# Two of the last head's four softmax tiles turned by DMA instead of by TensorE, in a two-layer graph attention kernel

## The chip, the core and the metric

The kernel runs on one core of a Trainium2 chip. The metric is the device time of one execution in microseconds (us), as a median over several runs. TensorE (PE in the profile, its weight loads PEld), VectorE (DVE), ScalarE (ACT), GpSimd (POOL) and SyncE (SP) each work through their own list of instructions in order; SP here does nothing but issue DMAs. A wait on another engine or on a DMA holds up everything behind it on the same engine.

## What is computed

Two graph attention layers over 512 nodes and 16,896 edges, a residual and a normalisation. Cut to what matters:

```
def gat_layer(x, W, a_s, a_d, b, edges, concat):
    h = (x @ W).reshape(n, H, C)
    alpha_s, alpha_d = (h * a_s).sum(-1), (h * a_d).sum(-1)
    e = leaky_relu(alpha_s[src] + alpha_d[dst], 0.2)
    e = exp(e - segment_max(e, dst)[dst])
    alpha = e / (segment_sum(e, dst)[dst] + 1e-16)
    return segment_sum(h[src] * alpha, dst) + b

h   = elu(gat_layer(x, W1, ..., concat=True))   # 8 heads of 768
out = gat_layer(h, W2, ..., concat=True)        # 1 head of 768
return layernorm(x + out)
```

The kernel handles the edges densely: it counts the edges between each pair of nodes once, and a head's attention is then a 512x512 matrix, softmaxed row by row with the counts as weights, and multiplied with the head's features.

## The kernel before

**Tiles.** The 512 nodes are four tiles of 128 partitions. A softmax tile `q[t]` is 128 destinations x 512 sources, 32-bit floats. The product with the features wants sources on the partitions, so each of the four tiles has to be turned into its columns of the matrix `PT` (128 x 4 x 512).

**Order of the work.** The order on every engine is written out by hand; no scheduler moves anything. The loop at L833 runs seven times. Pass h multiplies head h's features with its attention (`mixed`, L742), applies the ELU, multiplies the result with head h's rows of W2 and adds that to the sum of layer two (`second`, L333). Beside this last product it makes the softmax of head h+1, and after it, except in the last pass, the features of head h+2. The products are split into halves with seven block products instead of eight (P1, P2, P6, P7, P4, P5, P3), each for two pieces of 128 rows. One piece is six matmul records of 128x384 in the trace, so each step n = 2 to 6 of L871 to L902 is twelve of them (m0, then m1, L305) and two VectorE evictions (e0, e1, L363).

**The softmax of a tile**, spread over these steps: `lift` (ACT, L452), `leak` (DVE, L456), `rank` (DVE row maximum, L461, then ACT exponential, L463), `weigh` (DVE, L667 to L673: times the counts, row sum, reciprocal, scaled).

**Two ways to turn a tile.** `turn` (L676) has TensorE transpose the four 128x128 blocks into a PSUM tile (L679; pool `tr`, two buffers), and ACT copies that to `PT` (L680). `turn_out` (L685) has ACT copy the tile apart into a plane of upper and a plane of lower half words (L687, tile `nr`, two buffers), and SP issues one DMA transpose of the 16-bit planes into a tile `zr` (L689, three buffers). `turn_in` (L691) has ACT interleave the half words of `zr` into `PT` (L692). Heads 0 to 6 and layer two use turn_out and turn_in for all four tiles, with the turn_in some steps later. The last head (number 7, made in pass h = 6, `last` in the code) uses `turn` for all four: tile 0 between the two pieces of step 4, tile 1 in step 5, tile 2 in step 6, and tile 3 ahead of the last two matmul records of step 6.

**What follows.** After that pass come, in program order, the loads of x (four DMAs on SP, L95) and of b2 (one on SP, L936), which are used by the last stage (L1027). Then `aggregate` (L706) multiplies the last head's features with `PT`: 48 matmul records of 128x512 (L710), each column group followed by ACT and DVE work, then `second` for the last head, layer two's own softmax, its product (L1039) and the normalisation. The first matmul of L710 waits for ACT's last write to `PT`.

Of the kernel before, what the change touches and what calls it, by code (L numbers as in the profile page):

```python
# [36 lines left out]
def gat_pass(  # L37
# [45 lines left out]
    def row_bcast(ap_row):  # L83
        return bass.AP(tensor=ap_row.tensor, offset=ap_row.offset, ap=[[0, P], [1, D]])
# [36 lines left out]
    def load_w1(h, slot="w2"):  # L121
        return load_w(W1, h, slot, w1[:, h * D:(h + 1) * D])

    def load_w2(h, slot="w1"):
        return load_w(W2, h, slot, w2[h * D:(h + 1) * D, :])

    def load_a(h, a_s, a_d):
        A[h] = []
        for name, a in (("a_s", a_s), ("a_d", a_d)):
            v = wpool.tile([P, D], F32, name=name)  # L130
            nc.sync.dma_start(v, row_bcast(a))
            A[h].append(v)
# [147 lines left out]
    def left(aT, s):  # L280
        a11, a12 = aT[:, :HK, :HN], aT[:, HK:, :HN]
        a21, a22 = aT[:, :HK, HN:], aT[:, HK:, HN:]
        tt = nc.vector.tensor_tensor
        return dict(P1=a11, P2=a12, P3=s[:, 2], P4=a22, P5=s[:, 0], P6=s[:, 1], P7=a21), [
            lambda: tt(s[:, 0], a21, a22, op=ALU.subtract),
            lambda: tt(s[:, 1], s[:, 0], a11, op=ALU.subtract),
            lambda: tt(a21, a11, a21, op=ALU.subtract),
            lambda: tt(s[:, 2], a12, s[:, 1], op=ALU.add),
        ]
# [23 lines left out]
    def half_logits(h, t):  # L313
        return [lambda al=al, a=a, sign=sign: nc.vector.scalar_tensor_tensor(
            scr, HS[h][:, t, :], sign, a, op0=ALU.mult, op1=ALU.mult, accum_out=al[:, t:t + 1])
            for al, a, sign in zip(AL[h], A[h], (1.0, -1.0))]
# [132 lines left out]
    def lift(h, t):  # L449

        q = qpool.tile([P, N], F32, name="q")
        nc.scalar.activation(q, BC[h][:, :N], AF.Identity, bias=AL[h][1][:, t:t + 1], scale=-1.0)  # L452
        return q
# [21 lines left out]
    if not general:  # L475
# [99 lines left out]
        for n, batch in enumerate(batches):  # L575
# [29 lines left out]
            if n + 1 == len(batches):  # L605
                spread(0)
                q = [lift(0, t) for t in range(NT)]
# [11 lines left out]
    else:  # L619
# [26 lines left out]
        q = [lift(0, t) for t in range(NT)]  # L646
# [17 lines left out]
    def weigh(q, t, scale=True):  # L664

        den = small.tile([P, 1], F32, name="den")
        nc.vector.scalar_tensor_tensor(q, q, 1.0, cnt[:, t, :], op0=ALU.mult, op1=ALU.mult,  # L667
                                       accum_out=den)
        rden = small.tile([P, 1], F32, name="rden")
        nc.vector.tensor_scalar(rden, den, EPS_DEN, None, op0=ALU.add)  # L670
        nc.vector.reciprocal(rden, rden)
        if scale:
            nc.vector.tensor_scalar(q, q, rden, None, op0=ALU.mult)  # L673
        return rden

    def turn(q, t):  # L676
        ps = tr.tile([P, 512], F32, name="tr")
        for s in range(NT):
            nc.tensor.transpose(ps[:, s * P:(s + 1) * P], q[:, s * P:(s + 1) * P], ident)  # L679
        nc.scalar.copy(PT[:, :, t * P:(t + 1) * P], ps[:, :N].rearrange("p (s d) -> p s d", d=P))  # L680
# [4 lines left out]
    def turn_out(q, t):  # L685
        apart = work.tile([P, N], F32, name="nr").bitcast(U16)
        nc.scalar.copy(apart.rearrange("p (h n) -> p h n", h=2), q.bitcast(U16).rearrange("p (n h) -> p h n", h=2))  # L687
        parted[t] = work.tile([P, N], F32, name="zr", bufs=3).bitcast(U16)
        nc.sync.dma_start(parted[t].rearrange("p (j d) -> p j d", d=P), apart, transpose=True)  # L689

    def turn_in(t):  # L691
        nc.scalar.copy(PT.rearrange("p s n -> p (s n)").bitcast(U16).rearrange("p (s n h) -> p s n h", s=NT, h=2)[  # L692
            :, :, t * P:(t + 1) * P, :], parted.pop(t).rearrange("p (h s d) -> p s d h", h=2, s=NT))
# [124 lines left out]
    def attended(k):  # L818


        b1_, b2_ = (wpool.tile([P, HK, HALF], F32, name=f"w2t{j}").rearrange("p k n -> p (k n)") for j in (2, 4))
        nc.sync.dma_start(b1_[:, :D], w2[(H - 1) * D + k * P:(H - 1) * D + (k + 1) * P, :])
        nc.sync.dma_start(b2_[:, :D], row_bcast(a_src2[0]))
        for b, cols in ((b2_, L), (b1_, R)):
            nc.sync.dma_start(b[:, D:], row_bcast(a_dst2[0])[:, cols])

        def times(cols, a, sign, out):
            return lambda: nc.vector.scalar_tensor_tensor(
                scr[:, cols], b1_[:, cols], sign, a, op0=ALU.mult, op1=ALU.mult, accum_out=out[:, k:k + 1])
        return [times(slice(0, D), b2_[:, :D], 1.0, V[:, :, 0]), times(L, b2_[:, D:], -1.0, V[:, :, 1]),  # L830
                times(R, b1_[:, D:], -1.0, V2)]

    for h in range(H - 1):  # L833
        if h + 2 < H:
            load_w1(h + 2)()
        else:
            A[H] = []
            for j, a in ((2, a_src2[0]), (4, a_dst2[0])):
                v = wpool.tile([P, HK, HALF], F32, name=f"w2t{j}").rearrange("p k n -> p (k n)")[:, :D]
                nc.sync.dma_start(v, row_bcast(a))  # L840
                A[H].append(v)
            last_sum = load_w2(H - 1, "w2")
        GA, gsums = left(gT, gS)
        finish = mixed(h, AA, BB, besides + [p for t in ((0, 1) if h else (0, 1, 3)) for p in half_logits(h + 1, t)])
        besides = []
        if h + 2 < H:
            load_a(h + 2, a_src1[h + 2], a_dst1[h + 2])
            attend = attended(h)
        pairs = second(h, GA, B2)
        for m, _ in pairs[:2]:  # L850
            m()
        pairs[0][1]()
        for f in finish:
            f()
        gsums[0]()
        pairs[1][1]()
        gsums[1]()
        if pending:
            pending.pop(0)()
        spread(h + 1)  # L860
        pairs[2][0]()
        gsums[2]()
        pairs[3][0]()
        gsums[3]()
        if pending:
            pending.pop(0)()
        pairs[2][1]()
        pairs[3][1]()
        last = h + 2 == H
        q = [lift(h + 1, 0)]  # L870
        for n in range(2, 7):  # L871
            (m0, e0), (m1, e1) = pairs[2 * n:2 * n + 2]
            m0()
            if not last:
                m1()
            if n < 6:
                leak(q[n - 2])
                rank(q[n - 2], n - 2)
            if n < 5:
                q.append(lift(h + 1, n - 1))  # L880
            if last:

                if n > 3:
                    turn(q[n - 4], n - 4)
                if n == 6:
                    weigh(q[3], 3)
                m1(lambda: turn(q[3], 3) if n == 6 else None)
            if not last and n == 6:
                turn_in(0)
                weigh(q[2], 2)  # L890
                turn_out(q[2], 2)
            e0()
            if last and 2 < n < 6:
                weigh(q[n - 3], n - 3)
            if not last and 3 < n < 6:
                weigh(q[n - 4], n - 4)
                turn_out(q[n - 4], n - 4)
            if not last and n == 6:
                weigh(q[3], 3)
                turn_out(q[3], 3)  # L900
                load_w2(h + 1)()
            e1()  # L902
        if h + 2 < H:
            B_, sums = right(W1[h + 2], "w2")
            pairs = projection(h + 2, XA, B_)
            for n in range(14):
                pairs[n][0]()
                if n == 0:
                    turn_in(1)
                    for f in attend:  # L910
                        f()
                    B2, sums2 = right(W2[h + 1], "w1")
                if n in (1, 3):
                    sums[n // 2]()
                if n == 1:
                    AA, sums3 = left_sums(h + 1)
                pairs[n][1]()
                if n in (2, 4):
                    turn_in(1 + n // 2)
                if n == 5:  # L920
                    BB, sums3 = right_sums()
                if 1 <= n < 9:
                    sums3.pop(0)()
                if n in (9, 10):
                    sums2.pop(0)()
                if n in (11, 13):
                    logits(h + 2, HS[h + 2], 2 + (n - 11) // 2)
        else:
            last_sum()
            B2, sums2 = right(W2[H - 1], "w1")  # L930
# [65 lines left out]
    q, rden = [lift(H, 0)], []  # L996
# [96 lines left out]
```

## Time and profile before

| | |
|---|---|
| median of 3 runs | 650.80 us (650.75 to 650.86) |
| profiled execution, its own time | 650.37 us |
| its span from first to last instruction | 648.6 us |
| busy PE / DVE / ACT / POOL | 98% / 80% / 43% / 7% of the span |
| DMA share in 549 to 557 us / 557 to 569 us | 0.03 / 0.08 |
| steps n = 4 to 6 of pass h = 6 on PE | 555.43 to 568.98 us |

Rows of the timeline are: start in us, length in us, engine, line, operation, output<-inputs, shapes, count, and in brackets the idle time of the engine just before and what ended it. Neighbouring instructions of one kind are merged in a row. A matmul's length contains its way through the array, so several overlap; what a group costs TensorE is read from the distance between the starts. PEclk is the granted TensorE clock, 1.00 in all stretches around the change.

### The profile page before, as it was taken

What the parts mean: (1) busy time and instruction counts of PE and PEld (TensorE: products, weight loads), DVE (VectorE), ACT (ScalarE), POOL (GpSimd) and SP (SyncE); (2) the same over time, 40 slices, a digit from 0 to 9 for tenths busy, and PEclk for the clock granted to TensorE, in tenths of its full rate; (3) what the DMA queues carried; (4) which work ended last, traced back from release to release, by engine and by line L of the source; (5) the groups of instructions that cost most, each with busy time, mean ns of one, the idle gap of its engine ahead of it and who ended that gap; (6) DMA issues with size and microseconds to landing.
All of it is one profiled execution on the core that took longest, in us unless ns stands there. A gap on an engine that the chain in (4) does not pass through costs nothing.

```text
span 648.6 us, 7216 instructions
## 1 busy us (share of the span) xinstructions
PE 637.7 (98%) x2383; PEld 405.0 (62%) x2383; DVE 519.6 (80%) x1141; ACT 277.3 (43%) x482; POOL 48.3 (7%) x90
## 2 busy tenths in 40 slices
PE   8999999999999999999999999999999999999995
PEld 4544586556765586556765586556755586644553
DVE  7989989977779677877779687877779687876775
ACT  6774744530726045430726045430726045243440
POOL 1310020011000110011000110011000110000000
PEclk9999999999999999999999999999999999999999
DMA  9993499197806792196806792196706892000122
GB/s 318 328 203 86 75 327 292 35 256 207 202 0 153 170 277 97 33 260 200 205 1 149 174 277 98 33 258 204 202 1 153 218 254 97 25 1 1 29 61 76
DMA packets 77640, 97.95 MB, mean 151 GB/s; under 512 B 37094, under 2 KB 60446, under 8 KB 77598
## 3 DMA queue, kind: packets, MB, share of 16 engines
q1 hardware_dynamic: 63934, 75.80, 37.5%
q0 software_dynamic: 12976, 20.65, 18.4%
q10 hardware_dynamic: 688, 0.98, 0.4%
q8 instruction: 21, 0.34, 0.2%
q14 instruction: 21, 0.17, 0.1%
HBM read 85.09 MB, written 1.57 MB: 134 GB/s over the span
## 4 chain that ended last, share of the span: by engine, by line
PE 96%; ACT 1%; DMA 1%; DVE 1%; issue 0%; SPq 0%
PE mm L305 64%; PE mm L764 20%; PE mm L710 3%; PE mm L1039 3%; PE held L305 2%; PE tr L543 1%; DMA w<-in_L_gnn_W_dram 1%; ACT os L515 1%; PE bc L446 0%; PE bc L543 0%; PE tr L963 0%; PE tr L679 0%; ACT xT L205 0%; DVE os L517 0%; PE bc L985 0%
## 5 line engine op out<-in xcount | busy, mean ns | idle before, releaser
L305 PE MATMUL mm<-w,gT 128*128 128x384 f32 x288 | 97.5, 488 | 0.0
L305 PE MATMUL mm<-w,xT 128*128 128x384 f32 x264 | 88.2, 488 | 0.0
L305 PEld LDWEIGHTS mm<-w,gT 128*128 128x128 f32 x288 | 54.0, 190 | 35.2 <-issue 1.6
L305 PEld LDWEIGHTS mm<-w,xT 128*128 128x128 f32 x264 | 50.0, 190 | 35.4 <-ACT os L515 0.8
L768 ACT COPY u<-mm 128x256 f32<-128x256 f32 x21 | 7.8, 372 | 142.0 <-PE mm L764 142.0
L463 ACT ACTIVATE q<-q,nmax 128x512 f32<-128x512 f32 x36 | 25.8, 721 | 89.8 <-DVE nmax L461 89.8
L764 PE MATMUL mm<-PT,hs 128*128 128x256 f32 x252 | 61.4, 380 | 0.0
L305 PE MATMUL mm<-w1t,gS 128*128 128x384 f32 x180 | 60.7, 486 | 0.0
L305 PE MATMUL mm<-w2t,xS 128*128 128x384 f32 x168 | 56.6, 487 | 0.0
L764 PEld LDWEIGHTS mm<-PT,hs 128*128 128x128 f32 x252 | 47.9, 190 | 8.3 <-issue 0.4
L363 DVE TENSOR_TENSOR h<-h,mm 128x384 f32<-128x384 f32 x72 | 39.7, 551 | 14.6 <-PE mm L305 14.0
L305 PEld LDWEIGHTS mm<-w1t,gS 128*128 128x128 f32 x180 | 34.2, 190 | 23.5
L305 PEld LDWEIGHTS mm<-w2t,xS 128*128 128x128 f32 x168 | 31.9, 190 | 22.4 <-ACT q L452 0.4
L764 PE MATMUL mm<-pS,gS 128*128 128x256 f32 x168 | 43.3, 380 | 0.0
L687 ACT COPY nr<-q 128x1024 uint16<-128x1024 uint16 x32 | 33.4, 1044 | 22.9 <-DVE q L673 15.8
L692 ACT COPY PT<-zr 128x1024 uint16<-128x1024 uint16 x32 | 37.1, 1160 | 2.0 <-DMA zr<-nr 2.0
L764 PEld LDWEIGHTS mm<-pS,gS 128*128 128x128 f32 x168 | 31.9, 190 | 4.7 <-DVE pS L737 0.4
L305 PE MATMUL mm<-w,gS 128*128 128x384 f32 x96 | 32.6, 486 | 0.0
L305 PE MATMUL mm<-w1t,gT 128*128 128x384 f32 x96 | 32.5, 488 | 0.0
L305 PE MATMUL mm<-w,xS 128*128 128x384 f32 x96 | 32.5, 488 | 0.0
L106 POOL DMA_DIRECT2D w1t<-in_L_gnn_W_dram x7 | 8.9, 1267 | 311.3 <-DVE hs L727 97.8
L363 DVE TENSOR_TENSOR u<-u,mm 128x384 f32<-128x384 f32 x28 | 15.4, 553 | 19.0 <-PE mm L305 18.7
(189 smaller groups left out, 1086.1 us busy)
## 6 DMA issues: line engine op xcount, KB each, us to landing
w<-in_L_gnn_W_dram SPq DMA_DIRECT2D x90, 384.0 KB, 6.1
w<-in_L_gnn_W_dram POOLq DMA_DIRECT2D x16, 576.0 KB, 9.5
w2t<-in_L_gnn_W_dram SPq DMA_DIRECT2D x10, 576.0 KB, 4.9
w1t<-in_L_gnn_W_dram SPq DMA_DIRECT2D x9, 576.0 KB, 4.6
w2t<-in_L_gnn_W_dram POOLq DMA_DIRECT2D x8, 576.0 KB, 9.8
w1t<-in_L_gnn_W_dram POOLq DMA_DIRECT2D x7, 576.0 KB, 8.7
a_s<-in_L_gnn_a_src_dram SPq DMA_DIRECT2D x8, 384.0 KB, 3.7
a_d<-in_L_gnn_a_dst_dram SPq DMA_DIRECT2D x8, 384.0 KB, 4.1
```

What stands on the lines that cost most here:

```text
L106: nc.gpsimd.dma_start(t1, upper[:, :, R], accum_op=ALU.add)
L305: nc.tensor.matmul(ps[:, :HALF], A_[p][:, k, i * P:(i + 1) * P], B_[p][:, k, :], start=start and k == 0, stop=k == HK - 1, skip_group_chec ...
L363: nc.vector.tensor_tensor(a, a, ps, op=ALU.subtract if p == "P7" else ALU.add)
L463: nc.scalar.activation(q, q, AF.Exp, bias=nmax, scale=-1.0)
L515: nc.scalar.activation(o, nodes, AF.Sign, bias=nidx[:, c:c + 1])
L543: nc.tensor.matmul(cps[t][r:r + B, :N], od[:, at[c] + b - blocks[c][0], :], h_, start=todo[b] == hits[b], stop=todo[b] == 1, tile_position ...
L687: nc.scalar.copy(apart.rearrange("p (h n) -> p h n", h=2), q.bitcast(U16).rearrange("p (n h) -> p h n", h=2))
L692: nc.scalar.copy(PT.rearrange("p s n -> p (s n)").bitcast(U16).rearrange("p (s n h) -> p s n h", s=NT, h=2)[:, :, t * P:(t + 1) * P, :], p ...
L710: nc.tensor.matmul(ps[:, :N], HS[h][:, s, c * P:(c + 1) * P], PT[:, s, :], start=(s == 0), stop=(s == NT - 1))
L764: nc.tensor.matmul(bank[p][:, :HN], A_[p][:, k, c * P:(c + 1) * P], B_[p][:, k, :], start=over is None and k == 0, stop=k == 1, skip_group ...
L768: nc.scalar.copy(u, part("P1"))
L1039: nc.tensor.matmul(ps[:, :cols.stop - cols.start], PT[:, s, t * P:(t + 1) * P], h2[:, s, cols], start=(s == 2), stop=(s == 1))
```

## The change

Tiles 0 and 1 of the last head are turned by turn_out and turn_in; tiles 2 and 3 stay with `turn`. turn_out of tile 0 follows its `weigh` in step 3, that of tile 1 in step 4; turn_in of tile 0 stands in step 5, that of tile 1 in step 6, ahead of `turn` of tile 2. Nothing else is edited. The two DMA transposes thereby stand ahead of the loads of x and b2 in SP's list.

```
             if last:
-                if n > 3:
-                    turn(q[n - 4], n - 4)
+                if n > 4:
+                    turn_in(n - 5)
+                if n == 6:
+                    turn(q[2], 2)
                 if n == 6:
                     weigh(q[3], 3)
                 m1(lambda: turn(q[3], 3) if n == 6 else None)
...
             e0()
             if last and 2 < n < 6:
                 weigh(q[n - 3], n - 3)
+                if n < 5:
+                    turn_out(q[n - 3], n - 3)
```

## The prediction

> **What bounds the kernel now.** I read the page first: busy shares, then the chain that ended last.
>
> ```profile
> span 648.6 us, 7216 instructions
> ...
> PE 637.7 (98%) x2383; PEld 405.0 (62%) x2383; DVE 519.6 (80%) x1141; ACT 277.3 (43%) x482; POOL 48.3 (7%) x90
> ...
> PE 96%; ACT 1%; DMA 1%; DVE 1%; issue 0%; SPq 0%
> ```
>
> TensorE is the bound: 98% busy, 96% of the chain. Time taken off its queue counts in full, unless what it feeds on is late. So next comes the timeline of PE around the four turns, where the distance between starts gives the price of each.
>
> ```profile
> 551.56 4.03 PE L305 MATMUL mm<-w,gT 128*128 128x384 f32 x12
> 555.43 2.10 PE L305 MATMUL mm<-w1t,gT 128*128 128x384 f32 x6
> 557.36 0.60 PE L679 MATMUL tr<-ident,q 128*128 128x128 f32 x4
> 557.80 2.10 PE L305 MATMUL mm<-w1t,gT 128*128 128x384 f32 x6
> 559.74 2.10 PE L305 MATMUL mm<-w1t,gS 128*128 128x384 f32 x6
> 561.67 0.60 PE L679 MATMUL tr<-ident,q 128*128 128x128 f32 x4
> 562.11 2.10 PE L305 MATMUL mm<-w1t,gS 128*128 128x384 f32 x6
> ...
> 567.71 0.60 PE L679 MATMUL tr<-ident,q 128*128 128x128 f32 x4
> 568.15 0.81 PE L305 MATMUL mm<-w,gS 128*128 128x384 f32 x2
> 568.98 20.87 PE L710 MATMUL mm<-PT,hs 128*128 128x512 f32 x48
> ```
>
> The reader is to see three things. A step without a turn lasts 555.43 - 551.56 = 3.87 us, so 0.3225 us a record. A turn puts the next row 0.44 us later (557.36 to 557.80, 561.67 to 562.11). And the last two records start at 568.15 and need 0.645, so L710 could start at 568.80; it starts at 568.98, 0.18 late. The timeline of ACT tells why:
>
> ```profile
> 558.80 0.57 ACT L680 COPY PT<-tr 128x512 f32<-128x512 f32 x1
> 561.86 0.72 ACT L463 ACTIVATE q<-q,nmax 128x512 f32<-128x512 f32 x1 [2.49 <-DVE nmax L461]
> 562.49 0.57 ACT L680 COPY PT<-tr 128x512 f32<-128x512 f32 x1
> 566.62 0.58 ACT L680 COPY PT<-tr 128x512 f32<-128x512 f32 x1 [3.56 <-PE tr L679]
> 568.35 0.58 ACT L680 COPY PT<-tr 128x512 f32<-128x512 f32 x1 [1.15 <-PE tr L679]
> ```
>
> Tile 3's copy starts 0.64 us after its transposes start (567.71), ends at 568.93, and L710 follows 0.05 later. This entry, ACT's last write to PT, is the place that the change can spoil.
>
> **What goes.** Two turns leave TensorE: 2 x 0.44 = **0.88 us**. Two L680 copies of 0.57 us leave ACT; nobody waited for these two.
>
> **What comes.** Per tile one L687 copy, one DMA transpose and one L692 copy. The trace has 32 of each, from other heads:
>
> ```profile
> L687 ACT COPY nr<-q 128x1024 uint16<-128x1024 uint16 x32 | 33.4, 1044 | 22.9 <-DVE q L673 15.8
> L692 ACT COPY PT<-zr 128x1024 uint16<-128x1024 uint16 x32 | 37.1, 1160 | 2.0 <-DMA zr<-nr 2.0
> ```
>
> ```profile
> L689 SPq DMA_TRANSPOSE zr<-nr x32: 1232/1233/1360, 68.8 to 620.0; - x32
> ...
> DMA to landing us min/median/max: 3.0/3.1/3.5
> ```
>
> ACT so gets 2 x (1.04 + 1.16 - 0.57) = 3.3 us more work. In 549 to 569 us it is busy for 6.7 us of 20, so there is room; what matters is the order. In the changed list ACT does: L687 of tile 0, exponential of tile 2, lift of tile 3, L687 of tile 1, exponential of tile 3, L692 of tile 0, L692 of tile 1, then the two L680. I walk through it:
>
> - Tile 0 is scaled by DVE until 555.28 + 0.49 = 555.77. L687 runs 555.80 to 556.85. Behind it waits the exponential of tile 2, whose row maximum is only there at 557.56: free. SP issues at 556.87; landed by 559.9 to 560.4.
> - Tile 1 is scaled until 559.15 + 0.48 = 559.63. L687 runs 559.66 to 560.71. Behind it waits tile 3's exponential, whose maximum comes at about 561.45 (561.83 before, as DVE gets ahead by 0.3 at 559.94, see below): free. SP issues at 560.73; landed at **563.8 to 564.2**.
> - L692 of tile 0: 562.2 to 563.35. L692 of tile 1 waits for its landing: 563.8 to 565.0, at the latest 565.4.
> - On PE step 5 now starts at 559.30 and step 6 at 563.17. Turn 2 starts at 563.17 + 1.94 = 565.11, so its copy can't start before 565.75. Turn 3 starts at 565.55 + 4 x 0.3225 = 566.84, its copy at 567.48, and that ends at 568.06.
>
> So L710 starts at **568.10 instead of 568.98**: the 0.88 us arrive whole, and the 0.18 us ahead of L710 stay as they are. ACT's slack: for tile 3's copy to start on time, tile 2's copy (0.57) must start by 566.91 and L692 of tile 1 (1.16) by 565.75. A landing up to 5.0 us after the issue costs nothing; from there each us costs one.
>
> **DVE beside it.** VectorE has nothing added, but it must keep pace. The eviction at 559.94 had waited 0.30 for PE; it now starts at 559.63, where DVE is simply finished with tile 1. From there DVE runs without a gap: tile 2 is scaled by 563.64 (wanted at 565.11), the eviction that the second half of step 6 writes after runs 563.64 to 564.2 (wanted at 565.55), tile 3 is scaled by 565.71 (wanted at 566.84). The tightest has 1.1 us left, so DVE is not late next. If it were, the price would be the lateness itself.
>
> **SP's queue.** The two transposes stand ahead of five loads. The loads of x went out at 538.84 and now go out behind the second transpose, 560.73 + 1.23 = 561.96; b2, at 555.62 before, follows at about 563.7. With the longest landing of the x rows, 5.7 us, all is there by 570. First use is the addition on DVE at 622.5 (line 1027): 52 us of cover. Without it the price would be up to the 23 us by which x is delayed, so I price it at nothing. DMA was nearly idle (share 0.03 to 0.08) where the transposes now run, and PE holds its rate beside transposes: the 36 records of 609.26 to 620.87 take 11.61 us, 0.3225 a record, with four transposes issued from 610.7 to 620.0.
>
> **Behind L710** everything on the chain to 640.84 is PE, and the DVE and ACT work between hangs on PE's own rows, so it all moves by 0.88. The loads of the last W2 rows were issued by 522.6.
>
> **Unknown, from both sides.** Gain: by the records' own length a turn is 0.60 rather than 0.44, and the 0.18 ahead of L710 could go, if the first copies ran better: at most 2 x 0.60 + 0.18 = 1.38. Loss: ACT copies and landing in this new place; the nearest rows (3.0 to 3.5 us, the latter with weight loads issued right behind, in head 6's softmax at 497.2) say nothing lost, ordinary loads (5.7) say 0.7 lost. I take the transposes' own rows.
>
> **A rule against the change.** The Trainium skill, "VectorE: DVE Perf Modes", section "The three transpose paths", gives 390 ns for a 128x128 bf16 block on TensorE and 1309 ns by DMA, and its rules for kernel authors say to use TensorE where PSUM will do as destination, as it does here. A tile is eight half-word blocks; as an estimate by that page alone, 8 x 1309 ns = 10.5 us of landing would put tile 1 at 571.2, L710 at about 573.6, and the kernel 4.6 us slower. The trace's 3.1 us for the whole tile decide against it, and so does the fact that here TensorE is the bound and DMA is not.
>
> **The sum.** The profiled execution took 650.37 us with a span of 648.6; minus 0.88 gives 649.49. That execution lies 0.43 under the median of the runs, so against the median 650.80 I forecast **649.9 us**. A measurement of this kernel can tell about 0.2% (1.3 us) from no change, so the forecast itself, -0.14%, counts as "same".
>
> **Rivals.**
>
> 1. *Given back at the entry of L710 (0.12).* TensorE's queue gets shorter, but the last write to PT doesn't come earlier, as ACT is behind: a copy delayed, or a landing 5 to 6 us after issue. Then 0 to 0.88 is lost: 650.0 to 650.8. For it: ACT's list is in order, and two more waits for a DMA stand ahead of the two copies. Against: 0.7 us of slack ahead of tile 2's copy, 1.5 more behind it, by the rows.
> 2. *Slower (0.08): the second transpose shares the DMA engines with x.* The four loads (1.5 MB) are issued from 1.2 us behind it, while it is in flight. If it landed only with the last of them, at 561.96 + 1.45 + 5.7 = 569.1, L692 would end at 570.3, the copies at 571.4, L710 start at 571.45: 2.5 us late, 653.3. It eats gain from a landing 5.0 us after the issue, passes zero at 5.9, and is slower by over 0.2% from 7.2. For it: this order is new, and loads of that size take 5.7. Against: in head 6 seven weight loads went out right behind the last transpose, and the longest landing of all 32 is 3.5.
> 3. *More than worked out (0.04).* The 1.38 from above, 649.4; any more would need a stall to go that I don't see.
>
> That the change doesn't do what it says, and TensorE still turns all four, is excluded by the diff; that its gain is void because the turns were hidden speaks against the 0.44 us seen between the starts.
>
> **Chances.** The forecast's own case (0.7 to 1.05 gained) has 0.76, rival 1 0.12, rival 2 0.08, rival 3 0.04. Faster by over 0.2% is rival 3 alone, 0.04; slower by over 0.2% is rival 2 less its mild part, 0.07; within 0.2% is the rest, 0.89. The range runs from the largest gain, 649.4, to the whole gain given back, 650.8; rival 2 lies outside.
>
> **What would show it.** Right: in the stretch of step 4 to 6 no L679 row but two, L710 starting 12.67 us after the row that is at 555.43 now, against 13.55; L680 of tile 3 waiting for PE. Wrong: L680 of tile 2 or 3 following L692 without a wait; L692 of tile 1 waiting for its DMA beyond 5 us after the issue; a PE wait for DVE in step 6; anything on the chain by SP or DMA behind 570.

## The result and the profile after

The changed kernel takes **649.74 us** (median of 21 runs, 649.34 to 650.11) against 650.80 for the kernel before (21 runs, 650.36 to 651.04): ratio 0.9983, 95% interval 0.9977 to 0.9990. That is 1.06 us less, with 0.65 to 1.5 as the interval; 0.88 was forecast. The prediction put a difference under 0.2% down as no change; this one is 0.17%, and 21 runs of each kernel are enough for an interval that leaves no change out. The profiled execution has a span of 647.8 us, 0.8 less than before.

The page first, its busy shares and the chain that ended last:

```profile
PE 637.2 (98%) x2375; PEld 404.0 (62%) x2375; DVE 519.7 (80%) x1141; ACT 280.7 (43%) x484; POOL 47.2 (7%) x90
...
PE 96%; ACT 1%; DMA 1%; DVE 1%; issue 0%; SPq 0%
```

TensorE is still the bound, with eight records fewer; ACT has 3.4 us more, the 3.3 of the sum. The timeline of PE, around the steps from which two turns are gone:

```profile
555.45 4.04 PE L305 MATMUL mm<-w1t,gT 128*128 128x384 f32 x12
559.32 4.03 PE L305 MATMUL mm<-w1t,gS 128*128 128x384 f32 x12
563.19 2.10 PE L305 MATMUL mm<-w,gS 128*128 128x384 f32 x6
...
567.29 0.81 PE L305 MATMUL mm<-w,gS 128*128 128x384 f32 x2
568.13 12.28 PE L710 MATMUL mm<-PT,hs 128*128 128x512 f32 x28
```

Steps 4, 5 and 6 now start 3.87 us apart, as steps 3 and 4 did before. L710 starts 568.13 - 555.45 = 12.68 us after step 4, against 568.98 - 555.43 = 13.55: 0.87 us. I use this distance below for every kernel, since it is free of what varies between executions ahead of step 4 (its start lies anywhere from 555.3 to 555.8). The timeline of ACT in the same stretch:

```profile
555.82 1.05 ACT L687 COPY nr<-q 128x1024 uint16<-128x1024 uint16 x1 [0.82 <-DVE q L673]
...
559.69 1.05 ACT L687 COPY nr<-q 128x1024 uint16<-128x1024 uint16 x1 [0.78 <-DVE q L673]
...
562.12 1.14 ACT L692 COPY PT<-zr 128x1024 uint16<-128x1024 uint16 x1
563.84 1.17 ACT L692 COPY PT<-zr 128x1024 uint16<-128x1024 uint16 x1 [0.58 <-DMA zr<-nr]
565.76 0.59 ACT L680 COPY PT<-tr 128x512 f32<-128x512 f32 x1 [0.75 <-PE tr L679]
567.49 0.58 ACT L680 COPY PT<-tr 128x512 f32<-128x512 f32 x1 [1.14 <-PE tr L679]
```

All four added copies stand in time in which ACT waited anyway. Tile 1 is apart at 560.74, its transpose is issued at 560.76 and lands 3.06 us later, and L692 starts at 563.84. Both L680 still wait for PE (0.75 and 1.14 us), not for L692.

### The profile page after: what moved, and what is told of

Its sections match the earlier page's. It is cut to its first block, busy times and chain, and to the rows that moved or that the text cites. A ratio compares the mean times of both kernels' runs of the same rounds, so it can differ in the third digit from the quotient of the medians.

```text
span 647.8 us, 7205 instructions
## 1 busy us (share of the span) xinstructions
PE 637.2 (98%) x2375; PEld 404.0 (62%) x2375; DVE 519.7 (80%) x1141; ACT 280.7 (43%) x484; POOL 47.2 (7%) x90
## 4 chain that ended last, share of the span: by engine, by line
PE 96%; ACT 1%; DMA 1%; DVE 1%; issue 0%; SPq 0%
PE mm L305 65%; PE mm L764 20%; PE mm L710 3%; PE mm L1043 3%; PE held L305 2%; PE tr L543 1%; DMA w<-in_L_gnn_W_dram 1%; ACT os L515 1%; PE bc L446 0%; PE bc L543 0%; PE tr L967 0%; ACT xT L205 0%; DVE os L517 0%; PE tr L679 0%; PE bc L989 0%
## 5 line engine op out<-in xcount | busy, mean ns | idle before, releaser
L305 PE MATMUL mm<-w,gT 128*128 128x384 f32 x288 | 97.4, 487 | 0.0
L305 PE MATMUL mm<-w,xT 128*128 128x384 f32 x264 | 88.2, 487 | 0.0
L305 PEld LDWEIGHTS mm<-w,gT 128*128 128x128 f32 x288 | 53.9, 190 | 35.3 <-issue 1.6
L305 PEld LDWEIGHTS mm<-w,xT 128*128 128x128 f32 x264 | 49.9, 190 | 35.5 <-ACT os L515 0.8
L305 PE MATMUL mm<-w1t,gS 128*128 128x384 f32 x180 | 60.5, 486 | 0.0
L305 PE MATMUL mm<-w2t,xS 128*128 128x384 f32 x168 | 56.6, 487 | 0.0
L305 PEld LDWEIGHTS mm<-w1t,gS 128*128 128x128 f32 x180 | 34.2, 190 | 23.9
L687 ACT COPY nr<-q 128x1024 uint16<-128x1024 uint16 x34 | 35.5, 1044 | 24.5 <-DVE q L673 17.4
L305 PEld LDWEIGHTS mm<-w2t,xS 128*128 128x128 f32 x168 | 31.8, 190 | 22.4 <-ACT q L452 0.4
L692 ACT COPY PT<-zr 128x1024 uint16<-128x1024 uint16 x34 | 39.4, 1159 | 2.6 <-DMA zr<-nr 2.6
L305 PE MATMUL mm<-w,gS 128*128 128x384 f32 x96 | 32.6, 486 | 0.0
L305 PE MATMUL mm<-w,xS 128*128 128x384 f32 x96 | 32.5, 487 | 0.0
L305 PE MATMUL mm<-w1t,gT 128*128 128x384 f32 x96 | 32.4, 487 | 0.0
```

Source lines behind the costliest of these rows:

```text
L305: nc.tensor.matmul(ps[:, :HALF], A_[p][:, k, i * P:(i + 1) * P], B_[p][:, k, :], start=start and k == 0, stop=k == HK - 1, skip_group_chec ...
```

## The experiments

The theory: each turn costs TensorE 0.44 us and nothing else; what replaces it is hidden as long as ACT's last write to PT isn't late at the entry of L710. The rivals: hidden costs of the added copies and transposes; a gain from loading x later; transposes that land late. "Distance" is the start of L710 minus the start of step 4, from each kernel's profile. Ratio and "kernel before" are from runs on the same chip.

| kernel | distance, us | median, us (runs) | kernel before, us | ratio, 95% interval |
|---|---|---|---|---|
| before | 13.55 | 650.80 (21) | | |
| changed | 12.68 | 649.74 (21) | 650.80 | 0.9977 to 0.9990 |
| e1, tiles 0 and 1 not turned | 12.67 | 649.87 (11) | 650.92 | 0.9977 to 0.9995 |
| e2, tile 0 alone by DMA | 13.12 | 650.25 (10) | 650.92 | 0.9981 to 1.0000 |
| e3, tile 1 apart a step later | 14.05 | 651.25 (10) | 650.92 | 0.9996 to 1.0015 |
| e4, turn_in of tile 1 last | 13.74 | 650.95 (10) | 650.92 | 0.9991 to 1.0010 |
| e5, x between the transposes | 13.67 | 651.92 (8) | 650.75 | 1.0016 to 1.0037 |
| e6, three tiles by DMA | 13.54 | 650.56 (10) | 650.75 | 0.9987 to 1.0006 |
| e7, tile 3 turned earlier | 12.49 | 649.39 (11) | 650.75 | 0.9972 to 0.9990 |
| e8, tile 1 apart a little later | 13.00 | 649.95 (10) | 650.75 | 0.9981 to 0.9999 |
| e9, x by ScalarE's queue | 12.68 | 649.81 (10) | 650.71 | 0.9978 to 0.9996 |
| e10, before again | 13.56 | 650.76 (11) | 650.71 | 0.9991 to 1.0009 |
| e11, x ahead of everything | 12.67 | 649.72 (10) | 650.71 | 0.9975 to 0.9994 |

### What the change removes, without what it adds (e1)

```
-                if n > 4:
-                    turn_in(n - 5)
...
-                if n < 5:
-                    turn_out(q[n - 3], n - 3)
```

> Leaves out the turning of tiles 0 and 1 altogether: their columns of PT keep what head 6 left there, so the output is not the reference's. The loads of x are back where they were in the kernel before. Theory (the gain is TensorE's two turns, and all that the change adds is hidden): L710 starts 12.68 us after the row of step 4, as in the changed kernel, and the time is the changed kernel's, 649.7 to 649.9. Rival (the added copies and transposes cost something): it is faster than the changed kernel, L710 earlier than 12.6 us. Rival (part of the gain is that x is loaded later): it is slower than the changed kernel though its L710 starts at the same place.

PE from step 4 to L710:

```profile
555.59 4.03 PE L305 MATMUL mm<-w1t,gT 128*128 128x384 f32 x12
...
568.26 4.13 PE L710 MATMUL mm<-PT,hs 128*128 128x512 f32 x9
```

Distance 12.67, 649.87 us. Two turns for nothing bring just what two turns for four copies and two transposes bring: no cost of the added work is seen. And x is loaded at 539.0 here, as before the change, so the later loading is no part of the gain.

### One tile instead of two (e2)

```
-                if n > 4:
-                    turn_in(n - 5)
-                if n == 6:
-                    turn(q[2], 2)
+                if n == 5:
+                    turn_in(0)
+                if n > 4:
+                    turn(q[n - 4], n - 4)
...
-                if n < 5:
+                if n == 3:
```

> Only tile 0 by DMA, tiles 1 to 3 by TensorE. Theory (0.44 us a turn): L710 starts 13.11 us after the row of step 4 (before 13.55, changed 12.68), time 650.3. Rival (the gain comes from something that one tile does already, such as the loads of x going out later): nearly the whole gain, 649.8. Rival (only the second matters): 650.8.

PE from step 4 to L710:

```profile
555.79 4.03 PE L305 MATMUL mm<-w1t,gT 128*128 128x384 f32 x12
...
568.91 3.27 PE L710 MATMUL mm<-PT,hs 128*128 128x512 f32 x7
```

Distance 13.12, half of the way (0.43 of 0.87), 650.25 us. The gain goes by turns.

### The same instructions, one of them later (e4)

```
-                if n > 4:
+                if n == 5:
                     turn_in(n - 5)
...
                 m1(lambda: turn(q[3], 3) if n == 6 else None)
+                if n == 6:
+                    turn_in(1)
```

> As the changed kernel, but turn_in of tile 1 behind the copy of tile 3, ahead of L710: the same instructions in another order on ScalarE. Theory: L692 starts at 568.05 and L710 at 569.2, 1.1 us later than in the changed kernel and 0.25 later than before: 651.0. Rival (added copies are hidden wherever they stand): 649.7.

ACT's row ahead of L710 in this kernel, then PE's:

```profile
568.33 1.16 ACT L692 COPY PT<-zr 128x1024 uint16<-128x1024 uint16 x1
```

```profile
569.55 2.84 PE L710 MATMUL mm<-PT,hs 128*128 128x512 f32 x6 [1.09 <-ACT PT L692]
```

L692 now stands between the copy of tile 3 and L710, and PE's row shows the wait for it by name, 1.09 us. Distance 13.74, 650.95 us: the whole gain is gone, by the place of one copy.

### Where the slack ends (e8, e3)

Tile 1 is taken apart later, in e8 behind the exponential of tile 3, in e3 also behind turn_in of tile 0. The diff is that of e8; in e3 the two lines under `n == 5` stand the other way round:

```
-                if n > 4:
-                    turn_in(n - 5)
+                if n == 5:
+                    turn_out(q[1], 1)
+                    turn_in(0)
+                if n == 6:
+                    turn_in(1)
...
-                if n < 5:
+                if n == 3:
```

> As the changed kernel, but tile 1 is taken apart behind the exponential of tile 3, ahead of turn_in of tile 0: a smaller delay than in the run with turn_out one step later. Theory: apart at 563.15, landed at 566.25, half a us past the point from which the landing counts (565.75, or 565.95 as the other run had it), so L710 12.98 to 13.18 us after the row of step 4, time 650.1 to 650.3. Rival (a delay is free as long as it stays under 1 us): 12.68 and 649.7.

> As the changed kernel, but tile 1's turn_out one step later, behind turn_in of tile 0. Theory (a landing past 565.75 is paid one for one at the entry of L710): tile 1's half words are apart at 564.25, landed at 567.35, in PT at 568.45, the two copies of tiles 2 and 3 follow, L710 at 569.6: 1.5 us later than in the changed kernel and 0.6 later than before, so 651.3 to 651.5. Rival (the entry isn't what decides, TensorE's queue is): 649.7 as changed.

ACT in e8, then in e3:

```profile
566.50 1.16 ACT L692 COPY PT<-zr 128x1024 uint16<-128x1024 uint16 x1 [2.05 <-DMA zr<-nr]
567.57 1.07 ACT L680 COPY PT<-tr 128x512 f32<-128x512 f32 x2
```

```profile
567.55 1.16 ACT L692 COPY PT<-zr 128x1024 uint16<-128x1024 uint16 x1 [3.10 <-DMA zr<-nr]
568.61 1.07 ACT L680 COPY PT<-tr 128x512 f32<-128x512 f32 x2
```

In both the copies of tiles 2 and 3 no longer wait for PE but follow L692 at once. Counted from step 4 (555.69 and 555.68) tile 1 lands after 10.81 and 11.87 us, and L710 starts after 13.00 and 14.05: the landing is 1.06 later and L710 1.05. Past the slack it is paid one for one. Taking 12.68 as the floor, the slack ends 10.49 us after step 4, which is 565.94 on the clock of the changed kernel; the prediction said 565.75 on that of the kernel before, 0.02 earlier. The difference is that copies in a row start before the one ahead ends: L692 of 1.16 us is followed after 1.07 (e8) or 1.06 (e3), and two L680 of 0.58 take 1.07. Both medians lie somewhat below what was expected (649.95 against 650.1 to 650.3, 651.25 against 651.3 to 651.5), as do those of other variants; e10 comes back to this.

### A third tile (e6)

```
-                if n == 6:
-                    turn(q[2], 2)
...
                 m1(lambda: turn(q[3], 3) if n == 6 else None)
+                if n == 6:
+                    turn_in(2)
...
-                if n < 5:
+                if n < 6:
```

> As the changed kernel, but tile 2 by DMA too, its turn_in behind the copy of tile 3. Theory (the entry of L710 decides): TensorE saves another 0.44, but tile 2 is scaled at 563.53, apart at 564.6, landed at 567.7, in PT at 568.85: L710 at 568.9, 13.46 us after the row of step 4, so nearly the whole gain is given back: 650.7. Rival (TensorE's queue decides): 12.24 and 649.3.

ACT's last row ahead of L710, then PE's:

```profile
567.84 1.16 ACT L692 COPY PT<-zr 128x1024 uint16<-128x1024 uint16 x1
```

```profile
569.06 3.27 PE L710 MATMUL mm<-PT,hs 128*128 128x512 f32 x7 [1.33 <-ACT PT L692]
```

TensorE is free 0.44 earlier and waits 1.33 us for tile 2. Distance 13.54, as before the change, and 650.56 us. The third turn is worth 0.44 and costs 1.3: tile 2 is scaled at 563.7 here and needs 1.05 + 3.1 + 1.16 us from there, more than is left.

### The rest of the wait ahead of L710 (e7)

```
-            if between and k == HK - 1:
+            if between and k == HK - 2:
```

> As the changed kernel, but tile 3 is turned ahead of the last four matmul records of step 6 instead of the last two, so that its copy is done 0.65 us earlier against TensorE's queue. Theory (the 0.19 us ahead of L710 is its wait for that copy): they go, L710 12.48 us after the row of step 4, time 649.5. Rival (those 0.19 us are a fixed price of the change from L305 to L710): 12.68, 649.7. Should VectorE have tile 3 scaled later than 566.2, TensorE waits and it is slower.

PE, from the end of tile 3's turn on:

```profile
566.92 1.46 PE L305 MATMUL mm<-w,gS 128*128 128x384 f32 x4
568.21 4.03 PE L710 MATMUL mm<-PT,hs 128*128 128x512 f32 x9
```

The four records need 4 x 0.3225 = 1.29 us, and L710 starts 1.29 after them: the 0.19 are gone. Distance 12.49, and at 649.39 us the fastest kernel of this study, 0.9981 of the kernel before (0.9972 to 0.9990). Here the distance doesn't show all of the gain. The first record of L710 takes 0.592 us, as all the others do, where in the changed kernel, behind its wait, it takes 0.697; so from the start of L710 to the next L305 it is 20.60 us instead of 20.70, and TensorE is 0.29 us earlier there, not 0.19. Against the changed kernel, which wasn't run beside it, the intervals overlap; that it is faster is shown by the profiles only.

### Loads beside the transposes (e5, e9, e11)

In e5 the four loads of x stand between the two transposes:

```
                 if n < 5:
                     turn_out(q[n - 3], n - 3)
+                if n == 3:
+                    xr = load_x()
...
-    xr = load_x()
```

> As the changed kernel, but the four loads of x stand between the two transposes in SP's list, so that tile 1's transpose is issued while 1.5 MB of x is in flight. Theory (a transpose lands in 3.0 to 3.5 us whatever is beside it, and up to 5.0 us is free): landing at most 3.5, L710 12.68 us after the row of step 4, time 649.7 to 649.9. Rival (it shares the DMA engines with x and lands with it): landing of 4 to 6 us after the issue, seen in the wait of L692 for its DMA; past 5.0 us L710 gets later by the excess, up to 13.7, time up to 650.9.

The piece of e5's chain that is tile 1's transpose (start and length) and ACT's row for tile 1, then the busy time by stretch in e5 and in the changed kernel (the last two columns are the share of the DMA engines and GB/s):

```profile
561.03 6.15 DMA zr<-nr
```

```profile
567.21 1.16 ACT L692 COPY PT<-zr 128x1024 uint16<-128x1024 uint16 x1 [3.68 <-DMA zr<-nr]
```

```profile
560.00:562.00 2.00, 2.00 (x8) 1.21 (x7) 1.97 (x5) 1.25 (x2) 0.00 (x0) 1.00 1.04 355
```

```profile
560.00:562.00 2.00, 2.00 (x8) 1.21 (x7) 1.97 (x6) 1.25 (x2) 0.00 (x0) 1.00 0.02 3
```

The second transpose, issued at 561.03 with the DMA engines full (355 GB/s) instead of idle (3 GB/s), lands at 567.18: 6.15 us instead of 3.06. Distance 13.67. The first transpose, with the loads right behind it, lands in 3.5 us. So the rival holds for the landing. The median is worse than the distance says, and than the rival's 650.9: 651.92 us with 650.97 to 654.48, ratio 1.0016 to 1.0037; the profiled execution was the fastest of the eight. That the landing is longer still in the others is likely but not shown.

Was it the place in SP's own queue, or the engines? e9 has one DMA for the whole of x, from ScalarE's queue:

```
                 if n < 5:
                     turn_out(q[n - 3], n - 3)
+                if n == 3:
+                    xr = hpool.tile([P, NT, D], F32, name="hs")
+                    nc.scalar.dma_start(xr, x.rearrange("(t p) d -> p t d", p=P))
...
-    xr = load_x()
```

> As the changed kernel, but x is loaded by one DMA of 1.5 MB that ScalarE issues right behind taking tile 0 apart: in flight at the same time as in the run with x between the transposes (there tile 1 landed after 6.15 us and the time was 651.9), but in another queue. Theory A (the transpose stood behind x in SP's own queue): landing 3.0 to 3.6, L710 12.7 us after the row of step 4, 649.7 to 649.9. Theory B (transposes share the DMA engines with any load in flight): landing of 4 to 7 us, L710 at 13 to 15, time 650.1 to 652.

The transposes' line (issue times, then issue to landing), and ACT:

```profile
L689 SPq DMA_TRANSPOSE zr<-nr x2: 1429/1944/2458, 556.8 to 560.7; - x2
...
DMA to landing us min/median/max: 4.5/6.0/7.4
```

```profile
564.25 2.22 ACT L692 COPY PT<-zr 128x1024 uint16<-128x1024 uint16 x2 [2.15 <-DMA zr<-nr]
...
567.38 0.58 ACT L680 COPY PT<-tr 128x512 f32<-128x512 f32 x1 [0.43 <-PE tr L679]
```

Tile 0 lands after 7.4 us, tile 1 after 4.5: theory A is wrong, a load holds up transposes across queues. The Trainium skill says so too ("DMA: Bandwidth & Descriptors", section "Issuing engines are not separate DMA queues": whichever engine starts them, DMAs run on the same 16 DMA engines and interleave); these numbers agree. Tile 1's transpose also stands behind tile 0's, which landed only at 564.23, so what each adds to its 4.5 us isn't shown. Theory B's second half is wrong as well: nothing comes of it in the time. x went out at 555.73, 5 us ahead of the second transpose, so tile 1 is in PT at about 566.5, still early enough for tile 3's copy to wait for PE (0.43): distance 12.68, 649.81 us.

In e11 the loads of x stand ahead of both transposes too, but so early that they have long landed:

```
+        if last:
+            xr = load_x()
         q = [lift(h + 1, 0)]
...
-    xr = load_x()
```

> As the changed kernel, but the loads of x stand ahead of both transposes and ahead of step 2, where they were in time in the kernel before: landed by 550. Theory: as changed, landing of tile 1 in 3.0 to 3.6, L710 at 12.68, time 649.7 to 649.9: it is loads in flight that harm a transpose, not their place in the list. Rival (the place of x's loads is part of the gain): slower than the changed kernel by 0.2 or more.

The transposes' line in e11:

```profile
L689 SPq DMA_TRANSPOSE zr<-nr x2: 1233/1650/2068, 557.0 to 560.9; - x2
...
DMA to landing us min/median/max: 3.1/3.1/3.1
```

Tile 1's transpose lands in 3.1 us (the trace has no landing for tile 0's, but its L692, at 562.24, waits for nothing); distance 12.67, 649.72 us. Ahead in the list is no harm; in flight is.

### The kernel before, once more (e10)

No edit; a control.

> The kernel before, unchanged, as a control: every variant so far gained 0.16 to 0.30 us more against the kernel before than the distance of L710 from step 4 says. If that is how the runs are taken, this one is 0.2 us faster than itself; if it belongs to the variants, it is the same within 0.1.

650.76 against 650.71: the way of taking runs does not favour what is newly run. So the variants' medians lie below what their distance says: by 0.2 in the changed kernel (1.06 against 0.87), by 0.03 (e9) to 0.30 us (e7) in the others but e5. It is 0.05% at most, below what the intervals can tell, and its cause stays open. Part of e7's 0.30 is the 0.10 named there. The rest isn't in the work behind the turns: from the start of L710 to ScalarE's last row every profiled kernel takes 74.5 us, the same within 0.02 (e7 0.1 less). What varies from one profiled execution to the next, by more than the 0.2 in question, is the start of step 4 and the time from that last row to the end of the span, in which the output is stored (4.9 to 5.5 us).

## Why the prediction was right, step by step

The mechanism that was forecast is the one that the runs show, and the distance of L710 is off by 0.01 us. The time has a part that isn't the forecast's: of the 1.06 us by the medians the mechanism gives 0.87, and the 0.2 that brought 649.74 instead of 649.9 are unexplained (e10).

- **TensorE's price, 0.44 us a turn.** Right: 0.87 us by the distance for two, 0.43 for one (e2), and the same without any replacement (e1). The row's length of 0.60 us would have given 1.2; the distance between starts is what counts for an engine whose records overlap.
- **ACT's order.** The walk held to within 0.1 us at every row: tile 0 apart from 555.82 (555.80 said), tile 1 from 559.69 (559.66), L692 of tile 1 at 563.84 (563.8), last copy at 567.49 (567.48), L710 at 568.13 (568.10).
- **The landing of 3.0 to 3.5 us.** Right with 3.06, though on fewer rows than was said: the trace of the kernel before has a landing for 25 of its 32 transposes. The estimate of 10.5 us that went with the Trainium skill ("VectorE: DVE Perf Modes", section "The three transpose paths") is far off for this shape: one instruction turns the whole tile of eight half-word blocks in the time given there for little more than two.
- **Slack of 5.0 us at the entry.** Nearly right: it ends 0.17 us later than said (e8 and e3). The sum had added whole durations of copies that overlap by 0.1 us each. Rival 1's "1.5 more behind" tile 2's copy was a misreading of the walk itself, which gives 567.48 - 565.75 - 0.57 = 1.16; ACT then waited 1.14 us there.
- **DVE.** Right: the eviction of step 4's second piece moved to 559.57 (559.63 said), tile 3 is scaled at 565.02 + 0.49 = 565.51 (565.71 said), 1.3 us ahead of its turn. The 0.2 come mostly from records that overlap here too: the eviction at 563.44 starts before the row ahead of it ends at 563.53.
- **x later, at nothing.** Right: e11 and e1 load it at 539 and have the same distance and time.
- **The 0.18 us ahead of L710.** Its cause, the last copy, is now shown: e7 takes it away, and with it 0.10 us more, so the wait cost 0.29 and the 0.18 was too small. It was taken into the lower end of the range as a thing that might go by itself; it did not.
- **Rival 1 (given back at the entry)** did not happen, but the mechanism is real and near: e4, e6 and e3 give back 1.06, 0.86 and 1.37 us of distance by it.
- **Rival 2 (transposes held up by loads)** did not happen in the changed kernel, where x goes out 1.3 us behind the second transpose. It is real where loads are in flight ahead of it: e5 is slower than before. The prediction had named loads behind the transpose; what decided is loads ahead of it. Loads right behind cost nothing that stands out: 3.06 us in the changed kernel, 3.5 in e5 and 3.7 in e2, while in e7 tile 0's took 3.65 with no load beside it.

## What to carry to other kernels

Where one engine is the bound, moving its small auxiliary work to idle engines pays what the distance between starts says, and only if the replacement, much longer in itself (5.3 us here for 0.44), ends before the next consumer asks: write down for each piece when its input is there, how long the chain is, and when it is wanted. Two of the four tiles had that time; the third did not, and moving it too gave everything back (the fourth, scaled later still, was not tried). A DMA on such a chain belongs ahead of bulk loads or so far behind them that they have landed, whichever queue they are in: with loads in flight its landing took 4.5 to 7.4 us here instead of 3.06.

## What the runs showed of the hardware beyond that

- A DMA transpose of a 128x1024 half-word tile landed in 3.0 to 3.7 us wherever the traces of these runs show a landing, but for three: in 6.15 us with 1.5 MB of loads ahead in its queue (e5), and in 7.4 and 4.5 us beside a 1.5 MB load of another queue (e9).
- ScalarE's DMA issue in e9 came at 555.73, while the copy ahead of it in the list ran from 555.72 on: the issue did not wait for the copy to end.
- Copies on ScalarE in a row overlap: 1.16 us and 0.58 us by their records, 1.06 and about 0.49 from start to start.
- The first matmul of L710 takes 0.697 us where TensorE has waited for PT, and 0.592 where it has not (e7).
